# Four graph layers in fp32: the projections by one level of Strassen's algorithm

## The chip, the core and the metric

The kernel runs on one NeuronCore of one Trainium2 chip. The metric is the device time of one execution in microseconds. The engines are TensorE (PE, with its weight loads PEld), VectorE (DVE), ScalarE (ACT), GpSimd (POOL) and SyncE (SP, which issues the loads and stores of x and adj here).

## The reference

The input x has 128 graphs of 128 nodes with 512 features, adj the 128 x 128 adjacency of each graph, all fp32. Four layers follow on each other, each of them `x = layernorm(x + layer(x))` over the features:

- layer 0: `relu(An x W + b)`, where An is A + I scaled by the inverse roots of its row sums on both sides
- layer 1: q and k (64 features each) from x, scores `q k^T / 8` times A, summed over a row; a softmax over the 128 nodes gives one weight per node, and the layer is that weight times `x Wv^T`
- layer 2: `relu([x, A x / deg] W^T)`, so a contraction over 1024
- layer 3: `An (x W + b)`, computed as `(An x) W + rowsum(An) b`

All weight matrices are 512 x 512 (that of layer 2 is 1024 x 512 and that of q and k 512 x 128).

## The kernel before

Four graphs are handled together as one group; 32 groups make the run. Nodes lie on the 128 partitions, so x of a group is a tile of 128 x 4 x 512. Two groups are in flight: iteration t of the main loop (L289) does layers 0 and 1 of group t beside layers 2 and 3 of group t - 1. The kernel is written for a tile framework: the source gives a program order and pools of buffers (a pool's tag has so many buffers, and a tile that wants one waits until an earlier user's last reader is done). A scheduler puts the instructions of each engine in order ahead of the run, by its own estimate of when each is ready: the first in program order among the ready ones goes next, and later ones are put forward only into gaps. On the chip each engine then runs its list in that order.

`prep` (L92) makes the two normalised adjacencies of a group, transposed on TensorE (L112, L117). `aggregate` (L132) multiplies a graph's x (stationary, in four chunks of 128 features) by such a matrix; the result, (A x)^T in chunks of features, lies in one PSUM bank and ScalarE copies it to SBUF (L138). `transpose_x` (L141) gives x^T in the same form (L145). `project` (L147) does a projection of one graph: four matmuls, or eight in layer 2, with a chunk of the left side as the stationary operand and 512 columns of the weight as the moving one, summed in one PSUM bank (L151). VectorE reads that bank, adds bias or residual and writes a new x tile (L184, L185 for layer 0, L248 for layer 1, L265 for layer 2, L278 and L279 for layer 3). `stats` (L159) takes mean and variance of a graph, `normalise` (L164) lets POOL raise the variance to the power -1/2 (L169) and VectorE scale the four graphs of the group in place (L171). Layer 1 has p_qk (L198), the scores (L212, L215) and two small transposes round the softmax (L221, L236). `row_sums` (L123) serves the bias of layer 3.

PSUM has eight banks: four for projections, two for aggregates, transposes, p_qk and scores, two for small results. x lives in a tile of its own after each layer, two buffers for each. Weights come by POOL's queue at the start (L66), x and adj by SP's (L55, L57).

Of the kernel before, what the change touches and what calls it, by code (L numbers as in the profile page):

```python
# [13 lines left out]
P = 128          # nodes of a graph, on the partitions  # L14
G = 4            # graphs handled together
F = 512          # features
C = F // P       # feature chunks of 128
ATT = 64
LN_EPS = 1e-5
DEG_EPS = 1e-6  # L20


@with_exitstack
def kernel(
# [4 lines left out]
    w0: bass.AP,      # [F, F]   in, out  # L29
    b0: bass.AP,      # [F]  # L30
    wqkT: bass.AP,    # [F, 2 * ATT]
    wvT: bass.AP,     # [F, F]   in, out
    w2T: bass.AP,     # [2 * F, F] in, out
    w3: bass.AP,      # [F, F]   in, out
    b3: bass.AP,      # [F]
# [7 lines left out]
    xp = ctx.enter_context(tc.tile_pool(name="xp", bufs=2))  # L43
    ap = ctx.enter_context(tc.tile_pool(name="ap", bufs=2))
    tp = ctx.enter_context(tc.tile_pool(name="tp", bufs=4))
    sp = ctx.enter_context(tc.tile_pool(name="sp", bufs=4))
    ps_big = ctx.enter_context(tc.tile_pool(name="ps_big", bufs=4, space=bass.MemoryType.PSUM))
    ps_t = ctx.enter_context(tc.tile_pool(name="ps_t", bufs=2, space=bass.MemoryType.PSUM))
    ps_s = ctx.enter_context(tc.tile_pool(name="ps_s", bufs=2, space=bass.MemoryType.PSUM))

    st = {}          # (name, group) -> tile

    def load(t):
        a = ap.tile([P, G, P], FP, tag="adj", name=f"adj_{t}", bufs=3)
        nc.sync.dma_start(a, adj[t * G:(t + 1) * G].rearrange("g n m -> n g m"))  # L55
        xi = xp.tile([P, G, F], FP, tag="x0", name=f"x0_{t}")
        nc.sync.dma_start(xi, x[t * G:(t + 1) * G].rearrange("g n f -> n g f"))  # L57
        st["adj", t], st["x0", t] = a, xi

# [1 line left out]
    load(0)  # L61

    def weight(src, name):
        n, m = src.shape
        w = const.tile([P, n // P, m], FP, tag=name, name=name)
        nc.gpsimd.dma_start(w, src.rearrange("(c p) m -> p c m", p=P))  # L66
        return w

# [11 lines left out]
    w0_sb = weight(w0, "w0_sb")  # L80
    b0_sb = broadcast_row(b0, "b0_sb")
    wqk_sb = weight(wqkT, "wqk_sb")
    wv_sb = weight(wvT, "wv_sb")
    w2_sb = weight(w2T, "w2_sb")
    w3_sb = weight(w3, "w3_sb")
# [6 lines left out]
    def prep(t):  # L92
# [3 lines left out]
        rdeg = sp.tile([P, G], FP, tag="rdeg", name=f"rdeg_{t}")  # L96
        nc.vector.tensor_scalar(rdeg, deg, DEG_EPS, None, ALU.max)
        nc.vector.reciprocal(rdeg, rdeg)
        ar = ap.tile([P, G, P], FP, tag="ar", name=f"ar_{t}")
        nc.vector.tensor_tensor(ar, a, per_graph(rdeg), ALU.mult)  # L100

# [4 lines left out]
        an = ap.tile([P, G, P], FP, tag="an", name=f"an_{t}")  # L106
        nc.vector.tensor_tensor(an, a, ident[:, None, :].to_broadcast([P, G, P]), ALU.add)
        nc.vector.tensor_tensor(an, an, per_graph(d), ALU.mult)

        p_r = ps_t.tile([P, G, P], FP, tag="pt", name=f"p_ar_{t}")  # L110
        for g in range(G):
            nc.tensor.transpose(p_r[:, g, :], ar[:, g, :], ident)  # L112
        arT = ap.tile([P, G, P], FP, tag="arT", name=f"arT_{t}", bufs=3)
        nc.scalar.copy(arT, p_r)
# [4 lines left out]
        nc.vector.tensor_tensor(anT, p_n, per_graph(d), ALU.mult)  # L119
        st["arT", t], st["anT", t] = arT, anT  # L120

    # row sums of An, which carry the bias of layer 3
    def row_sums(t):  # L123
        p = ps_s.tile([P, P], FP, tag="psm", name=f"p_rs_{t}")
        for g in range(G):
            nc.tensor.matmul(p[:, g:g + 1], st["anT", t][:, g, :], ones, start=True, stop=True)  # L126
        rs = sp.tile([P, G], FP, tag="rs", name=f"rs_{t}")
        nc.vector.tensor_copy(rs, p[:, :G])
        st["rs", t] = rs

# [1 line left out]
    def aggregate(name, t, g, xin, aT):  # L132
        """(A x)^T in chunks of 128 features, [f, node]."""
        p = ps_t.tile([P, C, P], FP, tag="pt", name=f"p_{name}_{t}_{g}")
        for c in range(C):
            nc.tensor.matmul(p[:, c, :], xin[:, g, c * P:(c + 1) * P], aT[:, g, :], start=True, stop=True)  # L136
        s = tp.tile([P, C, P], FP, tag="aggT", name=f"{name}_{t}_{g}", bufs=6)
        nc.scalar.copy(s, p)  # L138
        st[name, t, g] = s

    def transpose_x(name, t, g, xin, dst):  # L141
# [3 lines left out]
        nc.scalar.copy(dst, p)  # L145

    def project(name, t, g, parts):  # L147
        """sum over (lhsT chunks, weight chunks) -> PSUM [node, F]."""
        p = ps_big.tile([P, F], FP, tag="pb", name=f"p_{name}_{t}_{g}")
        for i, (lhsT, w) in enumerate(parts):  # L150
            nc.tensor.matmul(p, lhsT, w, start=(i == 0), stop=(i == len(parts) - 1))  # L151
        return p

    def new_x(name, t):
        z = xp.tile([P, G, F], FP, tag=name, name=f"{name}_{t}")
        mv = sp.tile([P, G, 2], FP, tag="mv" + name, name=f"mv{name}_{t}", bufs=2)
        st[name, t], st["mv" + name, t] = z, mv

    def stats(name, t, g):  # L159
        s = sp.tile([P, 6], FP, tag="bn", name=f"bn{name}_{t}_{g}")  # L160
        nc.vector.bn_stats(s, st[name, t][:, g, :])  # L161
        nc.vector.bn_aggr(st["mv" + name, t][:, g, :], s)  # L162

    def normalise(name, t):  # L164
        z, mv = st[name, t], st["mv" + name, t]
        ve = sp.tile([P, G], FP, tag="ve", name=f"ve{name}_{t}")
        nc.vector.tensor_scalar(ve, mv[:, :, 1], LN_EPS, None, ALU.add)  # L167
        r = sp.tile([P, G], FP, tag="rstd", name=f"rstd{name}_{t}")
        nc.gpsimd.tensor_tensor(r, ve, nhalf, ALU.pow)  # L169
        for g in range(G):  # L170
            nc.vector.tensor_scalar(z[:, g, :], z[:, g, :], mv[:, g, 0:1], r[:, g:g + 1],  # L171
                                    ALU.subtract, ALU.mult)

# [1 line left out]
    def l0_agg(t, g):  # L175
        aggregate("agg0", t, g, st["x0", t], st["anT", t])

    def l0_out(t, g):
        a = st.pop(("agg0", t, g))
        p = project("o0", t, g, [(a[:, c, :], w0_sb[:, c, :]) for c in range(C)])  # L180
        if g == 0:
            new_x("x1", t)
        z = st["x1", t][:, g, :]
        nc.vector.tensor_tensor(z, p, b0_sb, ALU.add)  # L184
        nc.vector.scalar_tensor_tensor(z, z, 0.0, st["x0", t][:, g, :], ALU.max, ALU.add)  # L185
        stats("x1", t, g)

# [1 line left out]
    def l1_xT(t, g):  # L189
        if g == 0:  # L190
            st["xT1", t] = tp.tile([P, C, G, P], FP, tag="xT1", name=f"xT1_{t}", bufs=2)
        transpose_x("xT1", t, g, st["x1", t], st["xT1", t][:, :, g, :])

    def l1_qk(t):
        xT = st["xT1", t]
        p = ps_t.tile([P, G * P], FP, tag="pt", name=f"p_qk_{t}")
        for c in range(C):
            nc.tensor.matmul(p, wqk_sb[:, c, :], xT[:, c].rearrange("p g n -> p (g n)"),  # L198
                             start=(c == 0), stop=(c == C - 1))
        qT = tp.tile([ATT, G * P], FP, tag="qT", name=f"qT_{t}", bufs=2)  # L200
        kT = tp.tile([ATT, G * P], FP, tag="kT", name=f"kT_{t}", bufs=2)
        nc.scalar.mul(qT, p[0:ATT, :], 1.0 / ATT ** 0.5)
        nc.scalar.copy(kT, p[ATT:2 * ATT, :])
        st["qk", t] = qT, kT

    def l1_scores(t):
# [3 lines left out]
        for g in range(G):  # L210
            s = slice(g * P, (g + 1) * P)
            nc.tensor.matmul(p[:, g, :], qT[:, s], kT[:, s], start=True, stop=True)  # L212
# [6 lines left out]
    def l1_softmax(t):  # L219
        p = ps_s.tile([P, P], FP, tag="psm", name=f"p_w_{t}")  # L220
# [13 lines left out]
    def l1_weights(t):  # L234
        p = ps_s.tile([P, P], FP, tag="psm", name=f"p_ws_{t}")
# [5 lines left out]
    def l1_v(t, g):  # L241
        xT = st["xT1", t]
        st["v", t, g] = project("v", t, g, [(xT[:, c, g, :], wv_sb[:, c, :]) for c in range(C)])

    def l1_out(t, g):
        if g == 0:
            new_x("x2", t)
        nc.vector.scalar_tensor_tensor(st["x2", t][:, g, :], st.pop(("v", t, g)), st["ws", t][:, g:g + 1],  # L248
                                       st["x1", t][:, g, :], ALU.mult, ALU.add)
        stats("x2", t, g)  # L250

# [1 line left out]
    def l2_in(t, g):  # L253
        aggregate("agg2", t, g, st["x2", t], st["arT", t])
        s = tp.tile([P, C, P], FP, tag="xT2", name=f"xT2_{t}_{g}", bufs=3)
        transpose_x("xT2", t, g, st["x2", t], s)
        st["xT2", t, g] = s

    def l2_out(t, g):
        xT, a = st.pop(("xT2", t, g)), st.pop(("agg2", t, g))  # L260
# [112 lines left out]
```

## Time and profile before

| what | value |
|---|---|
| runs, us | 2959.02, 2960.64, 2961.89; median 2960.64 |
| profiled execution, span us | 2958.7 |
| what lies between the profiled span and the median, us | 1.9 |
| granted TensorE clock, mean | 0.997 |
| PE busy, us, instructions | 2896.0, 10304 |
| PEld busy, us | 1568.0 |
| DVE busy, us, instructions | 1396.0, 3138 |
| ACT busy, us | 425.7 |
| POOL busy, us | 167.5 |
| L151 (projections): MATMUL instructions | 3072 + 1024 + 1024 |
| DMA traffic over the span | 28 GB/s; 255 GB/s in the first 35 us |
| first aggregate starts at, us | 34.6 |

The page gives the span of one profiled execution, from its first to its last instruction; its time is shown no other way, and the runs beside it include the little that lies round the span. "Busy" is the time in which an engine had an instruction under way; matmuls overlap in a pipeline, so the spacing of their starts is their price, and their lengths are longer. In the group rows, the operation is followed by its tile names (result first), its shapes, the count, the busy time, the mean length of one in ns, and the idle time of the engine just ahead with what ended it. PEclk is the granted clock in tenths.

### The profile page before, as it was taken

The numbers are of one execution on the slowest core, as the hardware profiler recorded it, in microseconds if no ns is written. First come the engines' busy times: TensorE is split into PE (matmuls) and PEld (weight loads), VectorE is DVE, ScalarE is ACT, GpSimd is POOL, SyncE is SP. The second block draws the span as 40 slices with busy tenths as digits, with TensorE's granted clock in tenths as the row PEclk, the third lists the DMA queues.
The fourth block names the chain that finished last, engine by engine and source line by source line (L and its number), as shares of the span: only waits on it lengthen the run. The fifth ranks groups of instructions, "written<-read, shape, count | busy, mean of one in ns | idle before, by whom it ended". The sixth has DMA issues, their size and how long they took to land.

```text
span 2958.7 us, 25787 instructions
## 1 busy us (share of the span) xinstructions
PE 2896.0 (98%) x10304; PEld 1568.0 (53%) x10304; DVE 1396.0 (47%) x3138; ACT 425.7 (14%) x801; POOL 167.5 (6%) x173
## 2 busy tenths in 40 slices
PE   5999999999999999999999999999999999999998
PEld 2555555555555555555555555555555555555554
DVE  2455444455444554444554445544445544455443
ACT  1111111111111111111111111111111111111110
POOL 1000000000000000000000000000000000000000
PEclk9999999999999999999999999999999999999998
DMA  4000000000000000000000100000000001000000
GB/s 139 18 29 32 18 18 32 29 32 23 13 33 29 32 32 18 18 32 29 32 19 18 32 29 33 32 18 18 32 29 32 18 18 32 29 32 15 15 1 29
DMA packets 52391, 83.18 MB, mean 28 GB/s; under 512 B 1648, under 2 KB 18032, under 8 KB 52272
## 3 DMA queue, kind: packets, MB, share of 16 engines
q1 hardware_dynamic: 50688, 75.50, 7.4%
q0 software_dynamic: 1584, 6.03, 0.6%
q8 instruction: 82, 1.34, 0.2%
q14 instruction: 37, 0.30, 0.0%
HBM read 47.97 MB, written 33.55 MB: 28 GB/s over the span
## 4 chain that ended last, share of the span: by engine, by line
PE 97%; DMA 1%; ACT 1%; DVE 1%; issue 0%; POOL 0%; SPq 0%; POOLq 0%; ACTq 0%; DVEq 0%
PE p_o L151 60%; PE p_v L151 15%; PE p_agg L136 12%; PE p_qk L198 4%; PE p_xT L144 3%; PE p_sc L212 1%; DMA adj<-in_adj_dram 1%; PE p_rs L126 1%; ACT agg L138 1%; PE p_an L117 0%; PE p_ar L112 0%; PE p_ws L236 0%; PE p_w L221 0%; DVE x L171 0%; DVE bnx L161 0%
## 5 line engine op out<-in xcount | busy, mean ns | idle before, releaser
L151 PE MATMUL p_o<-w_sb,agg 128*128 128x512 f32 x3072 | 1381.5, 594 | 0.1
L151 PEld LDWEIGHTS p_o<-w_sb,agg 128*128 128x128 f32 x3072 | 566.9, 190 | 630.2 <-issue 629.0
L138 ACT COPY agg<-p_agg 128x512 f32<-128x512 f32 x384 | 225.1, 586 | 1730.9 <-PE p_agg L136 1730.9
L151 PE MATMUL p_v<-wv_sb,xT 128*128 128x512 f32 x1024 | 466.5, 600 | 0.0
L151 PE MATMUL p_o<-w_sb,xT 128*128 128x512 f32 x1024 | 465.8, 593 | 0.0
L265 DVE SCALAR_TENSOR_TENSOR x<-p_o,x 128x512 f32<-128x512 f32 x128 | 88.5, 691 | 782.5 <-PE p_o L151 782.5
L161 DVE BATCH_NORM_STATS2 bnx<-x 128x6 f32<-128x512 f32 x512 | 348.2, 690 | 12.1
L171 DVE TENSOR_SCALAR x<-x,mvx,rstdx 128x512 f32<-128x512 f32 x512 | 245.2, 542 | 151.5 <-POOL rstdx L169 151.5
L136 PEld LDWEIGHTS p_agg<-anT,x 128*128 128x128 f32 x2048 | 259.5, 194 | 83.4 <-issue 83.4
L151 PEld LDWEIGHTS p_v<-wv_sb,xT 128*128 128x128 f32 x1024 | 186.9, 190 | 213.5 <-issue 209.0
L136 PE MATMUL p_agg<-anT,x 128*128 128x128 f32 x2048 | 265.8, 278 | 6.5 <-DVE x L171 3.8
L151 PEld LDWEIGHTS p_o<-w_sb,xT 128*128 128x128 f32 x1024 | 182.2, 190 | 169.3 <-issue 169.3
L169 POOL TENSOR_TENSOR rstdx<-vex,nhalf 128x4 f32<-128x4 f32 x128 | 129.3, 1010 | 2462.6 <-DVE vex L167 2462.6
L145 ACT COPY xT<-p_xT 128x512 f32<-128x512 f32 x256 | 144.7, 590 | 212.3 <-PE p_xT L144 212.3
L136 PEld LDWEIGHTS p_agg<-arT,x 128*128 128x128 f32 x1024 | 131.8, 191 | 62.4 <-issue 45.9
L184 DVE TENSOR_TENSOR x<-p_o,b_sb 128x512 f32<-128x512 f32 x128 | 88.3, 690 | 157.9 <-PE p_o L151 157.9
L278 DVE SCALAR_TENSOR_TENSOR x<-b_sb,rs,p_o 128x512 f32<-128x512 f32 x128 | 95.6, 747 | 140.8 <-PE p_o L151 140.8
L144 PE MATMUL p_xT<-ident,x 128*128 128x128 f32 x1024 | 144.1, 274 | 4.4 <-DVE x L171 4.4
L136 PE MATMUL p_agg<-arT,x 128*128 128x128 f32 x1024 | 138.2, 278 | 9.1 <-ACT agg L138 9.1
L144 PEld LDWEIGHTS p_xT<-ident,x 128*128 128x128 f32 x1024 | 120.8, 142 | 39.4 <-issue 30.5
L198 PE MATMUL p_qk<-xT,wqk_sb 128*128 128x512 f32 x256 | 115.2, 592 | 0.0
L162 DVE BATCH_NORM_AGGREGATE mvx<-bnx 128x2 f32<-128x6 f32 x512 | 90.3, 179 | 13.1
(54 smaller groups left out, 879.5 us busy)
## 6 DMA issues: line engine op xcount, KB each, us to landing
x<-in_x_dram SPq DMA_DIRECT2D x32, 1024.0 KB, 5.3
out_dram<-x SPq DMA_DIRECT2D x32, 1024.0 KB, 4.3
adj<-in_adj_dram SPq DMA_DIRECT2D x32, 256.0 KB, 2.8
w_sb<-in_L_gnn_W_dram POOLq DMA_DIRECT2D x1, 2048.0 KB, 20.3
w_sb<-in_L_gnn_kernel_dram POOLq DMA_DIRECT2D x1, 1024.0 KB, 8.7
wv_sb<-in_L_gnn_W_v_dram POOLq DMA_DIRECT2D x1, 1024.0 KB, 13.4
w_sb<-in_L_gnn_W_dram POOLq DMA_DIRECT2D x1, 1024.0 KB, 22.5
b_sb<-in_L_gnn_bias_dram POOLq DMA_DIRECT2D x1, 256.0 KB, 9.3
```

The source lines that it names most:

```text
L136: nc.tensor.matmul(p[:, c, :], xin[:, g, c * P:(c + 1) * P], aT[:, g, :], start=True, stop=True)
L138: nc.scalar.copy(s, p)
L144: nc.tensor.transpose(p[:, c, :], xin[:, g, c * P:(c + 1) * P], ident)
L145: nc.scalar.copy(dst, p)
L151: nc.tensor.matmul(p, lhsT, w, start=(i == 0), stop=(i == len(parts) - 1))
L161: nc.vector.bn_stats(s, st[name, t][:, g, :])
L162: nc.vector.bn_aggr(st["mv" + name, t][:, g, :], s)
L169: nc.gpsimd.tensor_tensor(r, ve, nhalf, ALU.pow)
L171: nc.vector.tensor_scalar(z[:, g, :], z[:, g, :], mv[:, g, 0:1], r[:, g:g + 1], ALU.subtract, ALU.mult)
L198: nc.tensor.matmul(p, wqk_sb[:, c, :], xT[:, c].rearrange("p g n -> p (g n)"), start=(c == 0), stop=(c == C - 1))
L265: nc.vector.scalar_tensor_tensor(st["x3", t][:, g, :], p, 0.0, st["x2", t][:, g, :], ALU.max, ALU.add)
L278: nc.vector.scalar_tensor_tensor(z, b3_sb, st["rs", t][:, g:g + 1], p, ALU.mult, ALU.add)
```

## The change

The projections take two graphs at a time as a product of 2 x 2 blocks. The left side has two block rows (graph 0 and 1 of the pair, r) and two block columns (the two halves of its 512 features); the weight has 2 x 2 blocks of 256 x 256. Strassen's algorithm in the form with 15 additions makes the four result blocks from seven products of such blocks in place of eight. A group has two pairs (q). The products are named by the weight block or sum they use: B11, B21, B22 and the sums T1 to T4, which are made once (`weight_sums`: T3 = B22 - T1, and so on, on VectorE for layer 0's weight, on POOL for the four others). The sums of the left side are made by POOL, four operations of 128 x 512 for each left side (`left_sums`), five left sides an iteration.

In `project` each product is, for each of the two pairs, two matmuls of 256 moving columns for each part. Three PSUM tiles of one bank hold the products, some of them added up in PSUM (g1 takes B11 and B21, v takes T2, T3 and T4, q_ takes T1 and B22), and VectorE makes the result blocks from them with five adds. The first product is also kept in SBUF (by ScalarE; in layer 0 by two VectorE operations that add the bias). `fin` adds a finished block to x. The statistics of the graphs with r = 1 are taken two products before the end (behind T4), those with r = 0 at the end; the normalisation itself goes from VectorE to ScalarE, with one more small VectorE operation.

Other parts of the change:

- x stays in one tile through all four layers, updated in place (tag "x", four buffers, which takes the place of five tags with two buffers each); layer 3's bias is added to x ahead of the projection (`l3_bias`).
- All left sides share the tag "left" with three buffers of a whole group; the sums have three buffers each. PSUM has five banks for projections and three for all the rest.
- `prep` is cut in two: `prep_rows` behind layer 2, `prep_transpose` behind layer 3's aggregates; its untransposed matrices have one buffer each.
- Layer 0's aggregates of the next group are made ahead of layer 3's projection. Layer 1's transposes, p_qk, scores and softmax are put between the products of layer 2 (`hooks`).
- Layer 0's weight comes by ScalarE's queue, the others by POOL's as before, each now in four transfers.

The order of the instructions is the scheduler's in both kernels; the source only gives a program order. The diff, cut to its core:

```diff
+B11, T1, B21, B22, T2, T3, T4 = range(7)
...
-    xp = ctx.enter_context(tc.tile_pool(name="xp", bufs=2))
+    xp = ctx.enter_context(tc.tile_pool(name="xp", bufs=4))
...
-    ps_big = ctx.enter_context(tc.tile_pool(name="ps_big", bufs=4, space=bass.MemoryType.PSUM))
-    ps_t = ctx.enter_context(tc.tile_pool(name="ps_t", bufs=2, space=bass.MemoryType.PSUM))
-    ps_s = ctx.enter_context(tc.tile_pool(name="ps_s", bufs=2, space=bass.MemoryType.PSUM))
+    ps_b = ctx.enter_context(tc.tile_pool(name="ps_b", bufs=5, space=bass.MemoryType.PSUM))
+    ps_t = ctx.enter_context(tc.tile_pool(name="ps_t", bufs=3, space=bass.MemoryType.PSUM))
...
+    def weight_sums(w, eng):
+        eng.tensor_tensor(w[:, T3], w[:, B22], w[:, T1], ALU.subtract)
+        eng.tensor_tensor(w[:, T1], w[:, T1], w[:, B11], ALU.subtract)
+        eng.tensor_tensor(w[:, T2], w[:, B22], w[:, T1], ALU.subtract)
+        eng.tensor_tensor(w[:, T4], w[:, B21], w[:, T2], ALU.subtract)
...
+    def left(name, t):
+        st[name, t] = tp.tile([P, G, C, P], FP, tag="left", name=f"{name}_{t}")
...
+        nc.scalar.copy(st[name, t][:, g], p)
...
+    def left_sums(name, t):
+
+        a = st[name, t].rearrange("p (q r) (h c) n -> p q r h c n", r=2, h=2)
+        a11, a12, a21, a22 = a[:, :, 0, 0], a[:, :, 0, 1], a[:, :, 1, 0], a[:, :, 1, 1]
+        s1, s2, s3, s4 = (tp.tile([P, 2, 2, P], FP, tag=f"s{i}", name=f"{name}s{i}_{t}", bufs=3) for i in (1, 2, 3, 4))
+        nc.gpsimd.tensor_tensor(s1, a21, a22, ALU.add)
+        nc.gpsimd.tensor_tensor(s2, s1, a11, ALU.subtract)
+        nc.gpsimd.tensor_tensor(s3, a11, a21, ALU.subtract)
+        nc.gpsimd.tensor_tensor(s4, a12, s2, ALU.subtract)
+        st[name, t] = {B11: a11, B21: a12, B22: s4, T4: a22, T1: s1, T2: s2, T3: s3}
...
+        def product(p, k, fresh):
+            for q in range(2):
+                for i, (left_, w) in enumerate(parts):
+                    for c in range(2):
+                        nc.tensor.matmul(p[:, q, :], left_[k][:, q, c, :], w[:, k, c, :],
+                                         start=(fresh and q == 0 and i == 0 and c == 0),
+                                         stop=(i == len(parts) - 1 and c == 1), skip_group_check=True)
+            if k in hooks:
+                hooks[k]()
...
+        g1 = region()
+        product(g1, B11, True)
+        sa, sb = first(g1, block)
+        v = region()
+        product(v, T2, True)
+        u2 = block("u2")
+        nc.vector.tensor_tensor(u2, v, sb, ALU.add)
+        product(g1, B21, False)
+        c11(g1, block)
+        product(v, T3, False)
+        u3 = block("u3")
+        nc.vector.tensor_tensor(u3, v, sb, ALU.add)
+        q_ = region()
+        product(q_, T1, True)
+        nc.vector.tensor_tensor(u3, q_, u3, ALU.add)
+        fin(1, 1, u3)
+        product(v, T4, False)
+        nc.vector.tensor_tensor(sa, v, sa, ALU.add)
+        fin(1, 0, sa)
+        norm_stats(name, t, 1)
+        product(q_, B22, False)
+        nc.vector.tensor_tensor(u2, q_, u2, ALU.add)
+        fin(0, 1, u2)
+        norm_stats(name, t, 0)
...
+    def norm_stats(name, t, r):
...
+        for q in range(2):
+            s = sp.tile([P, 6], FP, tag="bn", name=f"bn{name}_{t}_{r}_{q}")
+            nc.vector.bn_stats(s, z[:, 2 * q + r, :])
+            nc.vector.bn_aggr(mv[:, q, :], s)
...
+        nc.gpsimd.tensor_tensor(rstd, ve, nhalf[:, 0:2], ALU.pow)
+        nmr = sp.tile([P, 2], FP, tag="nmr", name=f"nmr{name}_{t}_{r}")
+        nc.vector.scalar_tensor_tensor(nmr, mv[:, :, 0], -1.0, rstd, ALU.mult, ALU.mult)
+        for q in range(2):
+            zg = z[:, 2 * q + r, :]
+            nc.scalar.activation(zg, zg, AF.Identity, bias=nmr[:, q:q + 1], scale=rstd[:, q:q + 1])
...
+        def first(p, block):
+            sa, sb = block("s"), block("sb")
+            nc.vector.tensor_tensor(sb, p, bias(1), ALU.add)
+            nc.vector.tensor_tensor(sa, p, bias(0), ALU.add)
+            return sa, sb
...
+    def l2_in(t):
+        left("agg2", t)
+        left("xT2", t)
+        for g in range(G):
+            aggregate("agg2", t, g, st["arT", t])
+            transpose_x("xT2", t, g)
+        left_sums("xT2", t)
+        left_sums("agg2", t)
...
+        project("o2", t, [(st.pop(("xT2", t)), w2x_sb), (st.pop(("agg2", t)), w2a_sb)],
+                copy_first, lambda p, b: fin(0, 0, p), fin, hooks)
...
     for t in range(NT + 1):
...
         if a:
...
+            l0_out(t)
         if b:
...
+            l2_in(u)
+
+        def scores():
+            l1_xT(t)
+            l1_qk(t)
+            left_sums("xT1", t)
+
+        if a and b:
+            l2_out(u, {B11: scores, B21: lambda: l1_scores(t), T1: lambda: l1_softmax(t),
+                       B22: lambda: l1_weights(t)})
...
+        if t + 1 < NT:
+            prep_rows(t + 1)
+        if a:
+            l1_out(t)
         if b:
...
+            l3_agg(u)
+            row_sums(u)
+            l3_bias(u)
+        if t + 1 < NT:
+            prep_transpose(t + 1)
+            l0_agg(t + 1)
         if b:
...
+            l3_out(u)
             store(u)
```

## The prediction

> **What bounds the kernel now.** I read the page's first two parts, then the chain of work that ended last, then TensorE's timeline in the middle of the run, then the groups with shapes kept apart.
>
> ```profile
> span 2958.7 us, 25787 instructions
> ...
> PE 2896.0 (98%) x10304; PEld 1568.0 (53%) x10304; DVE 1396.0 (47%) x3138; ACT 425.7 (14%) x801; POOL 167.5 (6%) x173
> ...
> PE   5999999999999999999999999999999999999998
> ...
> PEclk9999999999999999999999999999999999999998
> ```
>
> TensorE is busy in every slice but the first and last, at full granted clock. A busy PE need not be at its peak, so the chain and the timeline have to confirm it.
>
> ```profile
> PE 97%; DMA 1%; ACT 1%; DVE 1%; issue 0%; POOL 0%; SPq 0%; POOLq 0%; ACTq 0%; DVEq 0%
> PE p_o L151 60%; PE p_v L151 15%; PE p_agg L136 12%; PE p_qk L198 4%; PE p_xT L144 3%; PE p_sc L212 1%; DMA adj<-in_adj_dram 1%; PE p_rs L126 1%; ACT agg L138 1%; PE p_an L117 0%; PE p_ar L112 0%; PE p_ws L236 0%; PE p_w L221 0%; DVE x L171 0%; DVE bnx L161 0%
> ```
>
> The end is set by matmuls, 75% of it by the projections of L151, the very line that the change replaces. The next view is TensorE's timeline: start, length, then the group.
>
> ```profile
> 1442.43 1.95 PE L136 MATMUL p_agg<-anT,x 128*128 128x128 f32 x16
> 1444.21 3.70 PE L151 MATMUL p_o<-w_sb,agg 128*128 128x512 f32 x8
> 1447.75 1.05 PE L136 MATMUL p_agg<-anT,x 128*128 128x128 f32 x8
> 1448.64 3.60 PE L151 MATMUL p_o<-w_sb,agg 128*128 128x512 f32 x8
> 1452.08 1.05 PE L136 MATMUL p_agg<-anT,x 128*128 128x128 f32 x8
> 1452.97 7.03 PE L151 MATMUL p_o<-w_sb,agg 128*128 128x512 f32 x16
> 1459.84 1.05 PE L136 MATMUL p_agg<-arT,x 128*128 128x128 f32 x8
> ```
>
> Read starts against starts, since lengths overlap. Sixteen matmuls of 512 columns take 1459.84 - 1452.97 = 6.87 us, 429 ns each; eight of 128 columns take 0.89 us, 111 ns each. Every fp32 matmul of the source is two such instructions (3072 + 1024 + 1024 = 5120 in L151 for 128 graphs x 20 source matmuls = 2560). A weight load goes with each, and at 111 ns apart the loads still keep up with the stream. Successive first p_qk starts lie 90.54 us apart (1404.39 and 1494.93): one iteration of four graphs. In it L151 has 160 instructions, 160 x 0.429 = 68.6 us.
>
> **TensorE's saving.** One level of Strassen makes 7 products of half width out of 8: per layer and four graphs 7 products x 2 pairs x 2 chunks x 2 instructions = 56 instructions of 256 columns for 32 of 512; layer 2 twice that. Per iteration 5 x 56 = 280 for 160. The trace has no 256-column matmul; a line through (128, 111 ns) and (512, 429 ns) gives 217 ns, 280 x 0.217 = 60.8 us. Saving: 68.6 - 60.8 = 7.9 us an iteration, x 32 = **252 us**. Ends: exactly half of 429 would save 275 us. A price above the line has nothing in the trace for it, since loads keep up at half that spacing. I take 252. The other TensorE work (aggregates, transposes, p_qk, scores) keeps its number.
>
> **What the other engines get.** Prices from the groups with shapes kept apart (busy us, mean ns | idle before):
>
> ```profile
> L161 DVE BATCH_NORM_STATS2 bnx<-x 128x6 f32<-128x512 f32 x512 | 348.2, 690 | 12.1
> L138 ACT COPY agg<-p_agg 128x512 f32<-128x512 f32 x384 | 225.1, 586 | 1730.9 <-PE p_agg L136 1730.9
> L169 POOL TENSOR_TENSOR rstdx<-vex,nhalf 128x4 f32<-128x4 f32 x128 | 129.3, 1010 | 2462.6 <-DVE vex L167 2462.6
> L184 DVE TENSOR_TENSOR x<-p_o,b_sb 128x512 f32<-128x512 f32 x128 | 88.3, 690 | 157.9 <-PE p_o L151 157.9
> masks.py:199 POOL TENSOR_SCALAR_AFFINE_SELECT ident<-ident 128x128 f32<-128x128 f32 x1 | 0.3, 301 | 0.1
> masks.py:197 POOL MEMSET ident<- 128x128 f32 x1 | 0.2, 205 | 0.3 <-POOLq L361 0.3
> L361 POOL MEMSET const-float32-1.0<- 128x1 f32 x1 | 0.1, 105 | 0.0
> ```
>
> DVE, per iteration: 4 layers x (5 recombining adds + 4 results + 4 statistics) + 3 more in layer 0 + 4 bias operations = 59 operations of 512 elements at 0.69 us = 40.7 us. Small ones: 16 aggregates at 0.18, 16 of four elements or fewer at 0.17, preparation 3.9, scores and softmax 2.6, and 0.6 because layer 1's four results are eight halves: 12.7. Sum 53 us, against 1396/32 = 43.6 before; of an iteration of 84 us that is 63%. Not a bound on average.
> ACT: 26 copies at 0.59, the softmax 0.5 and 16 normalisations of 128x512, which leave DVE (from 0.59, the copy's price, to twice that): 25 to 35 us of 84. TensorE's work covers it.
>
> POOL gets 20 adds of 128x512 per iteration (L169's operation stays, 8 + 1 at 1.01 us), and the trace has no such add. Low end: the memset's slope, (205 - 105)/127 = 0.79 ns an element, gives 0.5 us. The affine select's slope, (301 - 105)/127 = 1.54, gives 0.9 us with one input; a second input at the same slope 1.7. High end: that plus all of L169's 1.01 us as fixed cost, 2.7 us. I take **1.3 us**, between one and two inputs; POOL is then at 20 x 1.3 + 9 = 35 us.
> [...]
>
> **New waits on TensorE's path.** Instructions are issued in the scheduler's order, so a wait holds everything behind it unless the scheduler put other work there.
> (a) Inside a layer three PSUM tiles take seven products; a product that adds to a tile waits until the last reader has gone. A one-part product lasts 8 x 0.217 = 1.74 us. VectorE's turnaround is 0.20 us (p_o to L184: TensorE goes on at 41.72, VectorE starts at 41.92) + 0.69 + about 0.1 = 1.0 us. Slack 0.7 us, one operation: hidden while VectorE is up to date, late when two are ahead.
> (b) VectorE is not up to date at a layer's end. From T4's end on it has two adds, two results and four statistics (8 x 0.69), four aggregates (0.18) and three small ones (0.17): 6.8 us, and T4 ends 1.7 us ahead of the layer's end plus 0.2 of lag, so it is done 5.3 us after the last product. Layer 0 of the next group follows layer 3 directly, and its B21 product waits for two VectorE reads of the first tile: 5.3 + 2 x 0.69 = 6.7 us, where TensorE wants it after two products, at 3.5. Of these 3.2 us the scheduler can fill most with layer 2's aggregates and transposes (16 x 0.111 x 2 + 16 x 0.110 = 5.3 us, their x long ready). I take 0.8. Layer 1 behind layer 2 wants T3 at 5.2 us and gets it at 5.3 + 0.7: 0.8 late, half filled: 0.4.
> (c) Layer 2's T2 needs the second sums of both operands: six POOL adds after the last copy, 0.8 + 6 x 1.3 = 8.6 us. Cover: product B11 16 x 0.217 = 3.5, 16 transposes x 0.110 = 1.8, p_qk 8 x 0.429 = 3.4: 8.7 us. Break-even, so 0.4 for what is misjudged.
> Sum 1.6 us x 31 = **50 us**; the low end is nothing, since these waits are new, and the high ends are the second and third rival. The old stalls, 90.54 less 168 x 0.429 + 112 x 0.111 + 42 x 0.110 = 89.1, are 1.4 us and stay.
> (d) Ends, once. The first group's T2 waits for two sums (1.7 us); 16 weight sums, 21 us of POOL, stand in front of a first power (I take 6, from 0 to 12); the last group's T2 in layer 2 lacks transposes and p_qk as cover: 8.6 - 3.5 = 5.1; layer 3 0.5 to 2. **15 us**. The first aggregate starts at 34.6 us because an(0) was put behind a degree sum that waits for the third adj load (the waits have p_an 25.8 us late): left as it is; without that 15 us are won, with 3 MB more in flight at 255 GB/s 12 are lost.
>
> **Sum.** Profiled span 2958.7; the median of the runs is 1.9 us above it. 2958.7 + 1.9 - 252 + 50 + 15 = 2773.6. I say **2770**.
>
> **Rivals.**
> - *All waits are covered* (0.2): speaks for it that before lost only 1.4 us an iteration under the same kind of scheduling. 2960.6 - 252 + 5 = 2714, with half price 2690.
> - *A buffer or a queue in the wrong order eats half* (0.2): the tag "left" has three buffers for four users. If layer 0's aggregate of the next group is put forward into a gap, it takes the one that the x transposes of layer 1 need, and these come only after layer 2, with transposes, p_qk, sums and softmax uncovered: some 3 to 5 us an iteration. For it: the start, where order cost 25.8 us. 2960.6 - 252 + 15 + 31 x 4.5 = 2863.
> - *POOL's adds are the bound of layer 2* (0.12): at T2, with price p, TensorE waits 0.8 + 6p - 8.7. The saving of 7.9 less the 1.2 of (b) is gone at p = 2.4 us, which lies inside my bounds. At 2.7 us: 8.3 a pass; 2960.6 - 252 + 31 x (8.3 + 1.2) + 25 = 3028: slower.
> - *The saving isn't there* (0.02): 256 columns at more than 245 ns would leave nothing; then 2960 to 3010.
>
> **Numbers.** Forecast 0.46, range of its own 2735 to 2815. The range of 8 in 10 takes in the first two rivals: 2690 to 2890. A measurement tells 0.2% (6 us) from no change. Faster: 0.46 + 0.2 + 0.2 = 0.86; of the last two, 0.01 falls within 0.2% and 0.13 is slower.
>
> **What would show it.** Right: 256-column starts 215 to 217 ns apart; iterations (p_qk to p_qk) at 84 us; POOL add near 1.3 us; TensorE's waits headed by L184-like reads and by sums, each under 1 us; VectorE near 53 us an iteration. Wrong: iterations over 86 us with p_xT behind layer 2 (second rival), or T2's weight loads waiting for POOL for more than 1 us a pass (third). A start of the first aggregate far from 34.6 us would move the sum by up to 15 us without touching the steps.

## The result: slower, 3024.8 us for 2960.0

The changed kernel takes 3024.81 us (median of four runs, 3021.87 to 3028.26), the kernel before on the same chip 2960.0 us: ratio **1.0218**, 95% interval 1.0204 to 1.0233. The forecast was 2770. The profiled execution has a span of 3026.5 us, against 2958.7.

The page of the changed kernel, with the lines that answer to those of before (busy times, TensorE's forty slices, the granted clock, the chain that ended last):

```profile
span 3026.5 us, 35469 instructions
...
PE 2743.8 (91%) x14144; PEld 2319.1 (77%) x14144; DVE 1775.0 (59%) x3750; ACT 849.4 (28%) x1409; POOL 1106.1 (37%) x969
...
PE   3999999999999999999999999999999999999996
...
PEclk9999999999999999999999999999999999999998
...
PE 54%; DVE 27%; POOL 10%; issue 5%; ACT 3%; DMA 1%; POOLq 0%; ACTq 0%; DVEq 0%
```

The slices show the same row of nines as before: a slice is 76 us, and waits of 1 to 2.5 us do not show in it. The chain does show them. Matmuls carried 97% of it before; now they carry 54%, and VectorE and GpSimd 37%, though neither is busy for more than 59%. So no other engine is a bound by its amount of work; the time is lost at moments at which TensorE waits for one of them.

**The account.** From the starts of all matmuls (512 columns at 429 ns, 256 at 216, 128 at 111, those of a column or four at what they took before) the span splits into issue and waits:

| us of the profiled span | before | after | difference | forecast |
|---|---|---|---|---|
| issue of TensorE | 2854.4 | 2593.5 | -260.9 | -252 |
| waits in the 30 iterations from the second p_qk on | 40.3 | 329.1 | +288.8 | +50 |
| ends: up to the second p_qk and behind the last, first matmul's start included | 52.5 | 91.0 | +38.5 | +15 |
| behind the last matmul's start | 11.5 | 12.9 | +1.4 | - |

So the saving arrived whole, and somewhat more than all of it was given back in waits. An iteration (p_qk to p_qk) went from 90.54 to 92.16 us: 81.05 us of issue in place of 89.2, and 11.1 us of waits in place of 1.3. These are the waits of one steady iteration, in order of time. They are taken from start to start; the idle times in the profile's lines are up to 0.2 us shorter, since a matmul's length is longer than its price (eight of 256 columns last 1.89 us below, from 1471.23 on, and the next start comes after 1.73).

| TensorE waits, us | what it waits for |
|---|---|
| 0.82 + 0.17 | p_ar's PSUM tile, held by rs's copy on VectorE |
| 1.36 | an aggregate's PSUM tile; ScalarE's copy stands behind a normalisation |
| 2.48 | layer 3's T3 product, for VectorE's u2 (L206) |
| 1.76 | ten matmuls right behind it, seven of them at 427 ns in place of 216, three at 283 to 358 |
| 0.38 | layer 0's B21 |
| 1.56 | layer 2's B11; ScalarE's xT copy stands behind two normalisations |
| 1.11 | layer 2's T2, for GpSimd's second sum of xT2 |
| 1.5 | the rest, none over 0.1 |

**The largest one.** T3 is added to the PSUM tile v, which the add that makes u2 has to read first (u_o in the profile, which leaves numbers out). TensorE's timeline through layer 3 of the middle of the run (start, length, then the group, the idle time before it and its releaser), the changed kernel:

```profile
1467.58 0.60 PE L191 MATMUL p_o<-w_sb,agg 128*128 128x256 f32 x2
1469.37 1.16 PE L158 MATMUL p_agg<-anT,x 128*128 128x128 f32 x8 [1.20 <-ACT agg L159]
...
1472.96 1.89 PE L191 MATMUL p_o<-w_sb,agg 128*128 128x256 f32 x8
1477.16 5.38 PE L191 MATMUL p_o<-w_sb,agg3s 128*128 128x256 f32 x16 [2.31 <-DVE u_o L206]
```

The B21 product at 1472.96 ends in time, T3 comes at 1477.16 only, and its sixteen instructions with T1's last 5.38 us where sixteen others take 3.6. VectorE's timeline of the same time says why u_o is late. GpSimd's follows, then the row of the first of the three preparation operations in the kernel before:

```profile
1467.22 4.18 DVE L371 SCALAR_TENSOR_TENSOR x<-b_sb,rs,x 128x512 f32<-128x512 f32 x3
1471.32 1.75 DVE L120 TENSOR_TENSOR ar<-adj,rdeg 128x512 f32<-128x512 f32 x1
1473.00 1.75 DVE L122 TENSOR_TENSOR an<-adj,ident 128x512 f32<-128x512 f32 x1
1474.78 1.63 DVE L123 TENSOR_TENSOR an<-an,d 128x512 f32<-128x512 f32 x1
1476.34 0.68 DVE L206 TENSOR_TENSOR u_o<-p_o,s_o 128x512 f32<-128x512 f32 x1
```

```profile
1468.46 1.73 POOL L176 TENSOR_TENSOR agg3s<-agg,agg3s 128x512 f32<-128x512 f32 x1
1471.23 1.29 POOL L173 TENSOR_TENSOR agg0s<-agg 128x512 f32<-128x512 f32 x1 [1.04 <-ACT agg L159]
1472.49 1.71 POOL L175 TENSOR_TENSOR agg0s<-agg 128x512 f32<-128x512 f32 x1
```

```profile
L100 DVE TENSOR_TENSOR ar<-adj,rdeg 128x512 f32<-128x512 f32 x32 | 21.9, 684 | 0.2
```

Two things meet here. The scheduler has put prep_rows (L120 to L123) of a group three further on (the 18th group's where layer 3 has the 15th) ahead of u_o: an urgent add stands behind three operations whose result TensorE reads an iteration later. And each of these takes 1.6 to 1.75 us, where the kernel before had 0.68 to 0.69 for the same. All three read two operands from SBUF while GpSimd makes its sums, and so do the three of L371 ahead of them: those take 1.84, 1.75 and 0.74 us, and the short one, from 1470.66 on, falls into GpSimd's idle time of 1.04 us. u_o, with one operand in PSUM, takes 0.68 beside GpSimd's sums too. The groups with shapes kept apart show the same for the whole run (busy us, mean ns), still the changed kernel:

```profile
L371 DVE SCALAR_TENSOR_TENSOR x<-b_sb,rs,x 128x512 f32<-128x512 f32 x128 | 157.9, 1272 | 0.1
L247 DVE SCALAR_TENSOR_TENSOR nmrv<-mvv,rstdv 128x2 f32<-128x2 f32 x64 | 77.2, 1206 | 38.0 <-POOL rstdv L245 38.0
L120 DVE TENSOR_TENSOR ar<-adj,rdeg 128x512 f32<-128x512 f32 x32 | 52.9, 1653 | 0.0
L247 DVE SCALAR_TENSOR_TENSOR nmro<-mvo,rstdo 128x2 f32<-128x2 f32 x192 | 31.9, 166 | 116.0 <-POOL rstdo L245 116.0
L176 POOL TENSOR_TENSOR agg3s<-agg,agg3s 128x512 f32<-128x512 f32 x32 | 55.2, 1725 | 0.0
L176 POOL TENSOR_TENSOR xT2s<-xT,xT2s 128x512 f32<-128x512 f32 x32 | 40.4, 1263 | 0.0
```

L247 is the plainest: an operation of two elements a partition takes 166 ns in three layers and 1206 in the fourth, where GpSimd's adds of 1.26 us run beside it. The loss is on both sides: GpSimd's fourth sum (L176) takes 1725 ns in layer 3 and 1263 for layer 2's xT.

**The two waits for ScalarE.** ScalarE's timeline ahead of the aggregate that waits 1.36 us, then ahead of the second half of layer 2's first product, the changed kernel:

```profile
1467.33 1.52 ACT L250 ACTIVATE x<-x,nmrv,rstdv 128x512 f32<-128x512 f32 x2 [1.92 <-DVE nmrv L247]
1468.76 1.53 ACT L159 COPY agg<-p_agg 128x512 f32<-128x512 f32 x3
...
1503.13 1.52 ACT L250 ACTIVATE x<-x,nmro,rstdo 128x512 f32<-128x512 f32 x2 [0.23 <-DVE nmro L247]
1505.13 1.52 ACT L250 ACTIVATE x<-x,nmro,rstdo 128x512 f32<-128x512 f32 x2 [0.47 <-DVE nmro L247]
1506.56 0.56 ACT L166 COPY xT<-p_xT 128x512 f32<-128x512 f32 x1
```

The xT copy at 1506.56 has had its data since 1502.7, when the transpose at 1502.12 ended. It waits in ScalarE's list behind four normalisations of layer 0 that themselves wait for VectorE and GpSimd. In the first case two normalisations of layer 1, held up by VectorE's small operation L247 (1.2 us beside GpSimd), stand ahead of the copies. ScalarE is busy for 28% of the run, and TensorE stands idle for 1.20 and 1.40 us for it here. GpSimd's sums start after these copies, so T2's 1.11 us comes of the same; experiment 5 tests it.

### The profile page after: what moved, and what is told of

Read it like the earlier page. It is cut to its first block, busy times and chain, and to the rows that moved or that the text cites. A ratio compares the mean times of both kernels' runs of the same rounds, so it can differ in the third digit from the quotient of the medians.

```text
span 3026.5 us, 35469 instructions
## 1 busy us (share of the span) xinstructions
PE 2743.8 (91%) x14144; PEld 2319.1 (77%) x14144; DVE 1775.0 (59%) x3750; ACT 849.4 (28%) x1409; POOL 1106.1 (37%) x969
## 3 DMA queue, kind: packets, MB, share of 16 engines
q0 software_dynamic: 1520, 4.98, 0.5%
## 4 chain that ended last, share of the span: by engine, by line
PE 54%; DVE 27%; POOL 10%; issue 5%; ACT 3%; DMA 1%; POOLq 0%; ACTq 0%; DVEq 0%
PE p_o L191 36%; PE p_v L191 11%; DVE bno L240 5%; DVE x L371 4%; PE p_qk L294 4%; POOL rstdo L245 2%; POOL rstdv L245 2%; ACT x L250 2%; DVE an L122 2%; DVE ar L120 2%; DVE s_o L217 2%; DVE x L262 1%; DVE x L377 1%; DVE x L342 1%; POOL xT2s L173 1%
## 5 line engine op out<-in xcount | busy, mean ns | idle before, releaser
L250 ACT ACTIVATE x<-x,nmro,rstdo 128x512 f32<-128x512 f32 x384 | 291.8, 807 | 911.5 <-DVE nmro L247 911.5
L191 PE MATMUL p_o<-w_sb,agg 128*128 128x256 f32 x1536 | 380.8, 384 | 7.9 <-DVE s_o L274 6.6
L191 PE MATMUL p_o<-w_sb,agg3s 128*128 128x256 f32 x1024 | 289.3, 441 | 69.7 <-DVE u_o L206 68.2
L191 PEld LDWEIGHTS p_o<-w_sb,agg 128*128 128x128 f32 x1536 | 280.8, 191 | 55.1 <-DVE s_o L274 18.6
L191 PEld LDWEIGHTS p_o<-w_sb,agg3s 128*128 128x128 f32 x1024 | 226.8, 224 | 121.3 <-issue 79.3
L206 DVE TENSOR_TENSOR u_o<-p_o,s_o 128x512 f32<-128x512 f32 x64 | 43.9, 685 | 456.2 <-PE p_o L191 456.2
L191 PE MATMUL p_o<-w2x_sb,xT2s 128*128 128x256 f32 x1024 | 271.2, 387 | 32.2 <-POOL xT2s L174 32.2
L191 PE MATMUL p_o<-w2a_sb,agg2s 128*128 128x256 f32 x1024 | 264.7, 381 | 0.7 <-POOL agg2s L174 0.7
L240 DVE BATCH_NORM_STATS2 bno<-x 128x6 f32<-128x512 f32 x384 | 250.2, 686 | 4.4
L191 PE MATMUL p_o<-w_sb,agg0s 128*128 128x256 f32 x1024 | 239.3, 382 | 3.6 <-POOL agg0s L174 3.6
L191 PE MATMUL p_v<-wv_sb,xT1s 128*128 128x256 f32 x1024 | 240.4, 382 | 0.0
```

Source lines behind the costliest of these rows:

```text
L191: nc.tensor.matmul(p[:, q, :], left_[k][:, q, c, :], w[:, k, c, :], start=(fresh and q == 0 and i == 0 and c == 0), stop=(i == len(parts) ...
L206: nc.vector.tensor_tensor(u2, v, sb, ALU.add)
L240: nc.vector.bn_stats(s, z[:, 2 * q + r, :])
L250: nc.scalar.activation(zg, zg, AF.Identity, bias=nmr[:, q:q + 1], scale=rstd[:, q:q + 1])
```

## The experiments

All ratios are against the kernel before, with the 95% interval behind.

**1. Row preparation held back.** prep_rows is issued only behind the u2 add of layer 2.

```diff
-        if t + 1 < NT:
-            prep_rows(t + 1)
+        if b and t + 1 < NT:
+            with tc.issue_after(st["u2", "o2"].ins):
+                prep_rows(t + 1)
```

> The three wide operations of prep_rows are tied behind layer 2's first recombining add, for the next group, where the scheduler had put them in front of layer 3's, two groups ahead. Nothing is left out. Theory (they make VectorE late for layer 3's T3, which costs 2.5 us and then about 4 us at half clock, 1.9 us): an iteration falls from 92.2 to about 87.8 us, the run to about 2890 us, and the granted clock stays at 1.0 in that stretch. Rival (TensorE is held up by ScalarE's normalisations and POOL's sums; T3 is late anyway because layer 3's bias alone keeps VectorE busy): under 1 us an iteration, 2995 us or more.

Measured: 2903.07 us, ratio 0.9806 [0.9791, 0.9821], 87.91 us an iteration. The wait at T3 and the half rate behind it are gone, the other waits stand as they were. L371 still takes 1268 ns. The iteration is 4.25 us shorter, so the order of VectorE's list is what the 2.48 and 1.76 us (4.24 together) hang on.

**2. Without GpSimd's sums of the left sides.** The products use the plain blocks in their place.

```diff
-        nc.gpsimd.tensor_tensor(s1, a21, a22, ALU.add)
...
-        st[name, t] = {B11: a11, B21: a12, B22: s4, T4: a22, T1: s1, T2: s2, T3: s3}
+        st[name, t] = {B11: a11, B21: a12, B22: a12, T4: a22, T1: a21, T2: a11, T3: a11}
```

> Left out: all left-side sums on POOL; each product reads a raw block in place of its sum, and TensorE's and VectorE's work stays. VectorE's order in front of layer 3's T3 stays as in the changed kernel. Theory (VectorE's operations with two SBUF inputs are slow because POOL adds at the same time): the four bias and three preparation operations fall from 1.3 to 1.7 us each to 0.7, T3 is in time, the clock stays up, T2 of layer 2 doesn't wait: an iteration of about 85 us, the run near 2800 us. Rival (the order alone makes T3 late, whatever POOL does): only T2's 1.1 us go, an iteration of 91 us, near 2990.

Measured: 2786.96 us (two runs), ratio 0.9412 [0.9393, 0.9430], 84.88 us an iteration. The groups of this kernel:

```profile
L366 DVE SCALAR_TENSOR_TENSOR x<-b_sb,rs,x 128x512 f32<-128x512 f32 x128 | 90.2, 747 | 0.1
L120 DVE TENSOR_TENSOR ar<-adj,rdeg 128x512 f32<-128x512 f32 x32 | 23.0, 719 | 0.0
```

The row preparation still stands ahead of u_o, and TensorE does not wait there: without GpSimd beside them the three operations take 2.1 us in place of 5.1. Taking away either the order or the contention removes this wait; neither alone would have made it. Of ScalarE's two waits the one at the aggregate falls from 1.36 to 0.29 us with GpSimd's sums gone, and the one at layer 2's first product stays, 1.31 for 1.56.

**3. Layer 2's first and second sums ahead of the third and fourth.**

```diff
-        left_sums("xT2", t)
-        left_sums("agg2", t)
+        left_sums("xT2", t, "agg2")
```

> POOL makes the second sums of both left sides of layer 2 before the third and fourth ones. Nothing is left out. Theory (layer 2's T2 waits for the sixth add of POOL's list): the 1.1 us wait at T2 goes, an iteration of 91 us, 2990 us. Rival (T2 waits for the late copies of ScalarE, POOL only passes it on): unchanged within 0.3 us an iteration, 3015 to 3030.

Measured: 3019.86 us, ratio 1.0194 [1.0177, 1.0211]. T2's wait is unchanged at 1.11 us: it is xT2's second sum that is late, and that one is the third of GpSimd's list in both orders. What is late is the copy ahead of the first.

**4. The new arrangement with plain products** of 512 columns, one graph at a time: in-place x, shared buffers, split preparation and ScalarE's normalisation stay, the sums go.

> The changed kernel's arrangement (x in place, shared buffers, normalisation on ScalarE, hooks, order) with plain products of 512 columns, 160 an iteration again, no sums and no recombining adds. Theory (the loss comes from the sums on POOL and from VectorE's recombining, not from the arrangement): close to the kernel before, 2950 to 3000 us, an iteration of 91 to 92 us. Rival (the arrangement itself, the normalisation in ScalarE's list and one set of buffers, holds TensorE up): the 5 to 6 us an iteration of ScalarE's waits stay, over 3080 us.

Measured: 2999.81 us, ratio 1.0131 [1.0116, 1.0146], 92.13 us an iteration. So the arrangement by itself cost 38 us, with no Strassen in it: the upper end of what the theory allowed, and far from the rival's 3080. Its waits are 2.9 us an iteration, and one of 1.91 stands between layer 2's transposes and aggregates, for a copy.

**5. Normalisations behind the copies.** Experiment 1, and ScalarE's normalisations of layer 0 are issued behind layer 2's last copy, those of layer 1 behind layer 3's copy of g1.

```diff
+        if name in ("o0", "v"):
+            later.append(scale)
+        else:
+            scale()
...
+        with tc.issue_after(st["copy", "last"].ins):
+            for f in later:
+                f()
```

> The kernel of the first experiment (row preparation held behind layer 2), and in it ScalarE's normalisations of layer 0 are held behind layer 2's last left-side copy and those of layer 1 behind layer 3's first copy, so that no copy stands behind a normalisation that waits for GpSimd's power. Nothing is left out. Theory (normalisations in front of copies make the waits of 1.36 and 1.56 us, and the late xT copies make layer 2's T2 wait of 1.11 us): these three go, 87.9 - 4.0 = 83.9 us an iteration, 2903 - 4.0 x 31 = 2780 us; if only the two copy waits go, 85.0 us and 2813 us. Rival (the copies are late because ScalarE has too much to do, not because of its order): the waits only move, 87 to 88 us an iteration, 2880 to 2910 us.

Measured: 2782.09 us, ratio **0.9398** [0.9384, 0.9412], 84.07 us an iteration. All three waits are gone (T2 waits 0.1 us), at the same ScalarE busy time, 853 us. The rival is out: ScalarE had time enough, and it was its order. (The bias operations of layer 3 take 763 ns on average in experiment 8, which has the same order of normalisations, 1268 in experiment 1 and 747 in experiment 2 without GpSimd's sums: the new order also moves them away from these.)

**6. Normalisations back on VectorE,** with experiment 1's order.

> The kernel of the first experiment with the normalisation back on VectorE, as in the kernel before (16 more operations of 128x512 an iteration, the small one that made the shift is gone). Nothing is left out. Theory (the two ScalarE waits come from the normalisation's place in ScalarE's order): they go, 2.9 us an iteration, but VectorE is later at each layer's end by two to four operations, 0.4 to 0.7 us each, at four layer ends, some of it in front of TensorE: 85 to 89 us an iteration, 2815 to 2935 us. Rival (the ScalarE waits are only ScalarE's load): no difference between this and the deferred version.

Measured: 2880.46 us, ratio 0.9727 [0.9707, 0.9747], 87.4 us an iteration. The two ScalarE waits are gone, and VectorE (1894 us busy for 1707 in experiment 5) is late in three other places: 1.86 us ahead of layer 0's aggregates, which wait for an adjacency behind the normalisation, and 1.41 and 0.94 in layer 1's transposes. The iterations vary from 86.6 to 87.9 us, and the mean granted clock of the four runs is 0.982 to 0.986, against 0.991 to 0.995 in experiment 1. With its order mended, ScalarE is better by 98 us (experiment 5); VectorE with an order mended for it was not run.

**7. Work added where TensorE waits:** twelve instructions of 256 columns, unread, between layer 3's B21 and T3 of the changed kernel.

```diff
+        if name == "o3":
+            idle = region()
+            for i in range(6):
+                nc.tensor.matmul(idle[:, i % 2, :], parts[0][0][B11][:, 0, 0, :], w3_sb[:, B11, 0, :],
+                                 start=True, stop=True, skip_group_check=True)
```

> The changed kernel with work added: six matmuls of 256 columns (twelve instructions, 12 x 0.216 = 2.6 us of TensorE) whose result nobody reads, in layer 3 between B21 and T3, where TensorE stands for 2.48 us and then runs nine matmuls at half rate. Theory (the half rate follows from TensorE standing idle): the added work lies in the wait, the clock stays whole there, and the iteration loses its 1.9 us of half rate: 92.16 - 1.9 = 90.3 us, 3025 - 1.9 x 31 = 2966 us, faster although work is added; the granted clock is 1.00 in the stretch after the wait. Rival (the half rate has another cause, such as the load on the other engines there): the clock falls all the same, and the time is 3025 us or up to 10 us more.

Measured: 2984.14 us, ratio 1.0072 [1.0055, 1.0088], 90.5 us an iteration: 41 us **less** than the changed kernel, with 12 x 32 instructions more. Stretches of time, with PEclk the eighth column (after the five engines' busy times): first the changed kernel, from the wait on, then this one, where the added work stands from 1452.05 to 1454.64.

```profile
1472.00:1477.00 5.00, 2.85 (x14) 2.16 (x12) 4.96 (x5) 0.02 (x1) 4.92 (x4) 1.00 0.00 0
1477.00:1482.00 5.00, 4.84 (x15) 4.01 (x16) 1.31 (x3) 0.00 (x0) 0.54 (x1) 0.66 0.00 0
```

```profile
1450.00:1455.00 5.00, 5.00 (x25) 4.36 (x24) 4.95 (x5) 0.00 (x0) 4.83 (x3) 1.00 0.00 0
1455.00:1460.00 5.00, 5.00 (x25) 4.41 (x24) 2.08 (x3) 0.00 (x0) 0.00 (x0) 1.00 0.00 0
```

The half rate is a granted clock of 0.66 over 5 us, and it goes when the wait is filled. The load on the other engines is the same in both (VectorE 4.96 and 4.95, GpSimd 4.92 and 4.83), so the wait itself was its cause. The mean granted clock of the four runs is 0.993 to 0.995, against 0.977 to 0.980 in those of the changed kernel.

**8. Experiments 5 and 3 together.**

> The fifth experiment with one more edit, that of the third: in layer 2 GpSimd makes the first and second sums of both left sides before the third and fourth. Nothing is left out. Theory (with the copies on time the second sum of the second left side, GpSimd's sixth add, is what T2 waits for only if T2 comes within 0.8 + 6 x 1.27 = 8.4 us of the last copy): a gain between 0 and 1 us an iteration on the fifth experiment, 0 to 31 us. Rival (GpSimd's order never mattered): the same time within 0.2 per cent.

Measured: 2775.18 us, ratio 0.9371 [0.9357, 0.9385]. The iteration is 84.04 us, that of experiment 5; the 7 us lie at the ends (6 us less by the account). In the steady state the order of the sums does not matter.

**9. The weight sums on VectorE,** in experiment 8.

```diff
-    for w in (wv_sb, w2x_sb, w2a_sb, w3_sb):
-        weight_sums(w, nc.gpsimd)
+    with tc.issue_after(st["first", "anT"].ins):
+        for w in (wv_sb, w2x_sb, w2a_sb, w3_sb):
+            weight_sums(w, nc.vector)
```

> The eighth experiment with the 16 weight sums of the four other weights made by VectorE, behind the first scaled adjacency, in place of GpSimd. Nothing is left out. Theory (at the start one VectorE operation stands still for 20.1 us, from 23.35 to 43.4 us, until GpSimd's unbroken train of 16 sums is over, and TensorE's first matmul waits for it at 43.3 us): the first matmul comes at 24 to 26 us, the first p_qk at 60 to 64 us in place of 75.4 (VectorE's own 16 sums, 16 x 0.6 = 10 us, now stand in front of layer 0's results), so 11 to 15 us less, 2760 to 2764 us. Rival (the operation waited for something else, such as a load): first matmul at 43 us, the same time.

Measured: 2765.46 us, ratio **0.9341** [0.9325, 0.9357], the best version here; 10 us less than experiment 8 by the medians (on another chip, where the kernel before is 1.3 us faster), 13.0 by the profiled spans. The first matmul starts at 23.9 us in place of 43.5, the first p_qk at 62.6 in place of 75.5. The row that explains it is VectorE's fourth wide operation on the first adjacency, here in experiment 8, then in experiment 5, whose instructions are the same up to there, then in this one:

```profile
23.35 20.08 DVE L130 TENSOR_TENSOR an<-an,d 128x512 f32<-128x512 f32 x1 [0.65 <-POOL d L122]
```

```profile
22.95 1.76 DVE L130 TENSOR_TENSOR an<-an,d 128x512 f32<-128x512 f32 x1
```

```profile
23.16 0.69 DVE L130 TENSOR_TENSOR an<-an,d 128x512 f32<-128x512 f32 x1 [0.65 <-POOL d L122]
```

In experiment 8 it stands still until GpSimd's train of 16 sums, from 23.30 to 42.85 us, is over. In the changed kernel it is a small operation (L113) that stands in the same train:

```profile
30.55 11.61 DVE L113 TENSOR_SCALAR dh<-deg 128x4 f32<-128x4 f32 x1
```

**10. Plain products with the mended order:** experiment 4 with the normalisations held back as in 5.

> The fourth experiment (the changed arrangement with plain products of 512 columns, one graph at a time, without any sums) with ScalarE's normalisations of layers 0 and 1 held back as in the fifth. Nothing is left out. Theory (its one large wait, 1.91 us an iteration, is that of layer 2's copies behind normalisations): 92.13 - 1.9 = 90.2 us an iteration, 3000 - 1.9 x 31 = 2941 us; against the eighth experiment this is then what the seven products bring once the order is mended, 2941 - 2775 = 166 us, or less than the 252 us forecast for TensorE alone by the waits and the ends that the sums bring. Rival (the wait is of another kind): 92 us an iteration and 3000 us as before.

Measured: 2936.89 us, ratio 0.9920 [0.9905, 0.9934], 90.08 us an iteration, 0.9 of it waits, so the wait of 1.91 us was that of the order. Against experiment 9 the seven products with their sums bring 2936.9 - 2765.5 = 171 us: 8.15 us of issue less 2.1 of waits in an iteration, x 31 = 187, less what the ends give back; with the order left to the scheduler they brought minus 25 (2999.8 to 3024.8).

## Why the prediction was wrong

**TensorE's saving** was right: 216 ns for 217, 261 us by the account for 252 (the line through two points was 1 ns high, 9 us over 8960 instructions).

**The prices of the other engines** were right where they ran alone: a GpSimd add 1.26 us (1.3 taken), GpSimd 1106 us in all (35 an iteration), ScalarE 27. VectorE's 55 us an iteration for 53 agrees by chance: without GpSimd's sums beside it (experiment 2) the same work takes 1550 us, 48 an iteration, and the rest is contention. The normalisation on ScalarE took 0.76 to 0.81 us, inside its bounds.

**Waits, the step that failed.** It gave 50 us; they were 289. The contention of VectorE with GpSimd got no term there: layer 3's bias operations take 1272 ns on average beside GpSimd's sums and 747 without them (experiment 2). Part by part:

- *(a), "hidden while VectorE is up to date, late when two are ahead".* The condition was right, and the sum gave it nothing, as if VectorE were up to date inside every layer. Six operations stood ahead of layer 3's u2 without a gap, moreover five of them at 1.63 to 1.84 us and not at 0.69. With the wait came a term that the sum had no line for, 1.76 us of half clock. Together 4.2 us an iteration; experiment 1 got 122 us back.
- *ScalarE: "TensorE's work covers it".* The share was a third, as predicted, and the conclusion did not follow: a normalisation that waited for a three-step chain through VectorE and GpSimd held every copy behind it. 1.36 + 1.56 us, and T2's 1.11 as a consequence: 4.0 us an iteration, and experiment 5 got 87.91 - 84.07 = 3.8 back.
- *(b)* gave 0.8 at layer 0's third product and 0.4 behind layer 2. Measured 0.38, and 0.14 in experiment 5: right in kind and smaller.
- *(c)* gave 0.4 at T2. With the copies on time (experiment 5) it is 0.1, so GpSimd's adds were covered, as the working had it.

**(d), the ends:** 38.5 us for 15. The train of weight sums was priced as a delay of a power, 6 us; it held VectorE out for 11.6 us, and the first aggregate started at 45.0 us for 34.6. In experiment 9, without it, the ends cost 14.3 us more than before, 13 less than in experiment 8.

**The rivals.** The time came out at the third rival's 3028 and not by its mechanism: the add's price was 1.26 us, far below the 2.4 from which it decides, and T2 waited 1.1 us, not 8.3; its sign, over 1 us a pass at T2, was met by the letter and by another cause. The second rival's sign was an iteration over 86 us with layer 1's transposes behind layer 2. They stand between layer 2's first two products, as the source has them: the wrong order was in VectorE's and ScalarE's lists, not in the buffers. So its title, "A buffer or a queue in the wrong order eats half", names what happened, while its working and its size do not fit.

With the order mended and the train gone, the account of experiment 9 is 2593.5 us of issue, waits in the iterations 89.5 (49 more than before, forecast 50), ends 66.8 (14 more, forecast 15) and 12.9 behind the last matmul's start: a span of 2762.6 and a median of 2765 us, 5 below the forecast. The forecast was that of a kernel whose queues are in a good order. That the two sums meet is in part chance, since 0.82 + 0.22 us of the remaining 3.0 an iteration is the wait at p_ar, which no step had. Why the scheduler put the preparation into layer 3 stays open; only that it did, and what it cost, is shown.

## What to carry to other kernels

When work moves from a full engine to idle ones, busy shares of the idle ones say nothing; write down, for each engine on the way, what stands in its list ahead of the operation that the full engine waits for, and what that in turn waits for. An engine's price taken alone was not its price beside another here: the three preparation operations took 1.63 to 1.75 us beside GpSimd's adds and 0.68 to 0.69 in the kernel before. So before GpSimd gets a steady load, list VectorE's operations that will run beside it, those with both operands in SBUF first, and work the sum out at both prices. And if a list is in the scheduler's hands, pin the few operations that can wait (preparation for later groups, normalisations) behind the urgent ones: two such pins were worth 243 us here.

## What the hardware showed

- *VectorE's operations on SBUF took longer beside GpSimd's adds.* In the iteration shown the operations of VectorE with two SBUF operands took 1.63 to 1.84 us beside these adds; the same groups have means of 699 to 747 ns in experiment 2, without them. The small operation L247 took 1206 ns on average beside them in the changed kernel and 161 in experiment 2. With one operand in PSUM u_o took 0.68 us beside an add, and the statistics average 679 to 686 ns with the sums and 682 to 687 without. One kind with a single wide operand was longer too: the normalisation of 128x512 on VectorE in experiment 6 took 0.54 us at the shortest and 1.49 at the longest, and two of them 2.90 us together (from 1387.89 on) beside GpSimd's adds from 1387.83 on. Two runs show an operation that stood for longer than one add of 1.25 us: 11.6 and 20.1 us, through a train of such adds. The second of them took 1.76 us in experiment 5, whose instructions are the same up to there, so the order of the instructions does not seem to settle which of the two happens; what does is not shown. The four runs of experiment 9, without the train, lie within 1.4 us of each other where those of experiments 5 and 8 spread over 8.7 and 6.2.
- *The clock fell after a short wait.* In the iteration shown, an idle time of 2.31 us in a busy stream was followed by 3.4 us at a granted clock of 0.50 (from 1477.5 to 1480.9), and idle times of 1.40 and 0.95 us, up to 1507.17 and 1511.94, by none (1.00 from 1505 to 1520). Nor was one of 1.75 us in experiment 4, up to 1484.18 of its run (the eight matmuls of 512 columns from 1485.61 on start 430 ns apart). Of the 30 iterations 29 have such a stretch, which makes 29 x 3.4 x 0.5 / 3026 = 0.016 of the 0.019 by which the mean clock of the run is lower (0.978 for 0.997). The length of a wait alone does not settle it: near the start of the changed kernel idle times of 1.38 and 0.82 us, up to 102.81 and 104.34, were followed by 3.4 us at 0.50 (105.4 to 108.8), and those of 1.40 and 0.95 us, up to 124.22 and 129.47, by none (1.00 from 122.8 to 132.0); in the kernel before 1.86 us, up to 83.80, was followed by none (1.00 from 83.8 to 90.0). Here a wait cost its own length and, where the clock fell, 1.76 us more in the iteration shown.
